# Two layers on a graph, one core: LayerNorm sums on GpSimd, the second unit turned later, the last two node tiles read first

## The chip, the cores and the metric

The kernel runs on one core of one Trainium2 chip. The metric is device time in microseconds of one execution, as the median of several runs; less is better. A NeuronCore has five engines with an instruction stream each: PE (matrix products, with a second queue PEld for the weight loads), DVE (VectorE), ACT (ScalarE), POOL (GpSimd) and SP (SyncE), which here issues nearly all DMAs. They run side by side and wait for each other by semaphores. Data lies in SBUF (128 partitions); PE writes its results to PSUM, from where DVE and ACT read them.

## What is computed

16 graphs of N = 1024 nodes with C = 256 channels, fp32. The inputs are `x` (16 x 1024 x 256), an adjacency `adj` (1024 x 1024) that all graphs share, and weights. There are two layers, and each ends in a residual sum and a LayerNorm over the channels:

```python
# layer 0
c_adj = mean(x, channels); diff = c_adj[:, None, :] - c_adj[:, :, None]
A   = abs(abs(sigmoid(diff) - 0.5) - 0.5) * 2.0
Wg  = adj * (A + A.T) * 0.5
q   = relu((x.T @ Wg) * para)                 # 4 heads of 64
k, v = split(x @ kv_w)
x   = layernorm(x + softmax(q k.T * scale) v)
# layer 1
h = relu(x @ w1_loop + adj @ (x @ w1_neigh) + b1)      # 256 -> 128
h = relu(h @ w2_loop + adj @ (h @ w2_neigh) + b2)      # 128 -> 256
x = layernorm(x + (x + h) * 0.5)
```

## The kernel before

The graphs are called batches, b = 0 to 15, and the program is a chain of them: while batch b is in its attention (layer 0), the first convolution of batch b-1 and the second of b-2 run between its parts, and the last LayerNorm of b-3. Each engine works strictly in the order in which the program text emits its instructions; nothing reorders them. A tile pool hands out buffers: 31 "row" buffers (128 x 1024 fp32) in SBUF go to one tile after the other in the order in which their last users stand in the program, and an instruction that writes a new tile waits for the last reader of the old one. PSUM is split in three "big" buffers (128 x 1024) and two "bank" buffers (128 x 512), also handed round; `half_psum` takes one half of a big one.

The large products use Strassen's scheme with seven products in place of eight, so that DVE, ACT and GpSimd have sums to prepare and to gather around each. An fp32 matmul takes two passes on PE, and both are shown as MATMUL rows.

The parts that matter here, in the order of one batch:

- **Attention, `Attention.both_units(pair)`.** A unit is a pair of heads by one half of the nodes; `both_units(0)` does units 0 and 1, `both_units(1)` units 2 and 3. `scores` multiplies kT and qT into eight tiles `s` (L757); ACT takes exp of each (L762, L764) into `pr`; DVE adds the eight up (`collect`, L776 and L778) and turns the sum in blocks of 32 x 32 to `accB` (`turned_sum`, L785). `part_sum` (L791) reduces `accB` to `den_part`, from which the softmax denominators come. `outputs` multiplies pr and v into a PSUM tile `av` (L803), which DVE turns to `o`: L828 for a pair's first unit, L835 for its second. With `summed` given (pair 0), `accB` is reduced ahead of the second unit's `outputs`; without it (pair 1) after L835.
- **`fast_inner` (L992 to L1022)**, between the two pairs: t1 = x1 times the first convolution's weights, for batch b-1, as seven products (L997) in the order 1, 2, 7, 6, 3, 4, 5, in three half PSUM tiles `upper`, `lower`, `chain`. DVE adds t1's first half behind product 2 (L1005), then runs `aside`, in most batches `turn_next`: the two transposes `xT` of the next batch's input (L253). After product 4 it adds the loop half (L1014), after product 5 L1016 and L1017, and turns t1 (L1018). Product 3 overwrites `upper`, which L1005 read. The next pair's scores take these PSUM tiles over: its first score tile the place of `upper`, its second that of `lower` (free after L1014), its fourth that of `chain` (free after L1017). Ahead of the products DVE prepares `X` by four subtractions (L984 to L987), and from batch 3 on `deviation_aside` (L1194).
- **`Joined.run`** does the two convolutions. Between its products DVE scales `o` by the denominators (L861), adds it to the blocked input xB (L863) and sums xB over 32 channels (`sum_output`, L866), and `join` (L290) adds the two halves of these sums.
- **The next batch's query products, `FastQueries`**: `times_adj` (L613) makes Wg, and four steps of seven products (L702) the query, each step over one quarter of a half's nodes. DVE gathers them in `end` (L713 and on).
- **`BlockedNorm`**, layer 0's LayerNorm, beside those steps. The data lies "blocked": partition p = (a, k), where the quarter a of 32 partitions holds other channels than its neighbour, and k stands for the node within a block of 32. A sum over all channels of a node so needs the four partition quarters added up. `fold_sums` does it by a matmul with a constant `fold` of ones on the right places (L286), whose result DVE reads from PSUM: `mean` (L356), subtracted in L359, and `variance` (L374), after ACT has squared and DVE has summed (L369, L290). GpSimd raises the variance to the power -1/2 (L376), and DVE scales with it (L381). The same `fold` adds the denominators up (L851).

For 13 batches, b = 2 to 14, the branch `elif both and more` (L1642) sets this order: `mean` goes between the fourth and fifth product of step 1, `variance` between the sixth and the last ones of step 3.

- **`ending` (L1213 to L1299)**: for the last batch the second convolution's result is finished by tiles of 128 nodes. `products` multiplies, `deviations` adds the residual (L1238), takes mean and variance (L325, L326), adds epsilon (L1241; on DVE for the last two tiles, on GpSimd for the others) and takes the power on GpSimd (L1242). Tiles 0 to 5 are normalised by ACT (L1249, `leave`), tiles 6 and 7 by DVE (L337), with one output DMA each (L1299). Their order on DVE: all of tile 6's `deviations`, all of tile 7's, then both normalisations.

Of the kernel before, what the change touches and what calls it, by code (L numbers as in the profile page):

```python
# [10 lines left out]
F32 = mybir.dt.float32  # L11
I32 = mybir.dt.int32
AF = mybir.ActivationFunctionType
ALU = mybir.AluOpType
# [4 lines left out]
def kernel(  # L19
# [31 lines left out]
    nc = tc.nc  # L51

    B, N, C = x.shape
    P = 128
    NT = N // P
# [14 lines left out]
    S = 32  # L70
# [212 lines left out]
    def fold_sums(part, name, psum_tile=bank_psum):  # L283

        pm = psum_tile(f"{name}_ps")
        nc.tensor.matmul(pm[:, 0:NB], fold.rearrange("p a k -> p (a k)"), part[:, 0, :], start=True, stop=True)  # L286
        return pm[:, 0:NB]

    def join(part):
        nc.vector.tensor_add(part[:, 0, :], part[:, 0, :], part[:, 1, :])  # L290

# [56 lines left out]
    class BlockedNorm:  # L348
# [2 lines left out]
        def __init__(self, xB, sums, name):  # L351
            self.xB, self.sums, self.name = xB, sums, name

        def mean(self):
            mean = small.tile([P, NB], F32, tag="mean", name=f"mean1_{self.name}", bufs=2)
            nc.vector.tensor_scalar_mul(mean, fold_sums(self.sums, f"sum1_{self.name}"), 1.0 / C)  # L356
            for cc in range(NC):
                x_cc = by_node(self.xB[cc])
                nc.vector.tensor_sub(x_cc, x_cc, mean.unsqueeze(2).to_broadcast([P, NB, S]))  # L359
# [9 lines left out]
                nc.vector.tensor_reduce(self.part[:, cc, :], by_node(self.sq[cc]), AX.X, ALU.add)  # L369
            join(self.part)  # L370

        def variance(self, psum_tile=half_psum):
            self.rstd = small.tile([P, NB], F32, tag="rstd1", name=f"rstd1_{self.name}", bufs=2)
            nc.vector.tensor_scalar(self.rstd, fold_sums(self.part, f"sum2_{self.name}", psum_tile), 1.0 / C, EPS,  # L374
                                    op0=ALU.mult, op1=ALU.add)
            nc.gpsimd.tensor_tensor(self.rstd, self.rstd, neg_half, ALU.pow)  # L376

        def scale(self):
# [350 lines left out]
    class Attention:  # L729
# [86 lines left out]
        def both_units(self, pair, first=lambda: None, second=lambda: None, third=lambda: None, summed=None):  # L816
            u = NJ * pair
            self.scores(u, 0)
            self.scores(u + 1, NT, summed=False)
            row = row_tile(f"o_{self.b}_{pair}")  # L820
            self.collect(u + 1, 1)
            first()
            self.collect(u + 1, 2, 3)
            second()
            self.outputs(u, half_psum, turned=False)
            self.collect(u + 1, 4, 5)
            pav, self.o[u] = self.o[u], row
            nc.vector.transpose(row[:, 0:FB], pav)  # L828
            self.collect(u + 1, 6, 7)
            accB = self.turned_sum(u + 1)  # L830
            if summed:
                summed()
                self.part_sum(u + 1, accB)
            self.outputs(u + 1, turned=False)
            nc.vector.transpose(row[:, FB:N], self.o.pop(u + 1))  # L835
            if not summed:
                self.part_sum(u + 1, accB)
            third()

        def add_pairs(self, *pairs):  # L840
            self.denominators(*pairs)
# [112 lines left out]
    class GraphConv:  # L954
# [258 lines left out]
        def ending(self, dst, quarters, aside, filled):  # L1213

            def bias(bank, *tiles):
                banks[tiles] = bank[:, 0:len(tiles) * C]
                for i, t in enumerate(tiles):  # L1220
                    banks[t] = bank[:, ts(i, C)]
                bank = bank[:, 0:len(tiles) * C].rearrange("p (i c) -> p i c", c=C)
                nc.scalar.copy(bank, b2_sb.unsqueeze(1).to_broadcast([P, len(tiles), C]))

            def products(*tiles):
                for t in tiles:
                    nc.tensor.matmul(banks[t], self.uT[:, ts(t, P)], w2n_sb, start=False, stop=False,
                                     skip_group_check=True)
                    nc.tensor.matmul(banks[t], self.h1T[:, ts(t, P)], w2l_sb, start=False, stop=True,
                                     skip_group_check=True)  # L1230

            def deviations(*tiles):
                n, rows = len(tiles), self.x[:, tiles[0]:tiles[-1] + 1, :]
                e = small.tile([P, 4 * per], F32, tag="mv_e", name=f"mv_e_{tiles[0]}", bufs=3)
                mv = e[:, 0:2 * n].rearrange("p (t s) -> p t s", s=2)
                rstd, shift = (e[:, (2 + k) * per:(2 + k) * per + n] for k in range(2))
                sums = banks[tiles[0]] if n == 1 else banks[tiles]
                nc.vector.scalar_tensor_tensor(rows, sums.rearrange("p (i c) -> p i c", c=C), 0.0, rows,  # L1238
                                               op0=ALU.max, op1=ALU.add)
                statistics(mv, rows, range(n), f"e{tiles[0]}")  # L1240
                (nc.vector if tiles[0] >= NT - 2 else nc.gpsimd).tensor_scalar_add(rstd, mv[:, :, 1], EPS2)  # L1241
                nc.gpsimd.tensor_tensor(rstd, rstd, neg_half[:, 0:n], ALU.pow)  # L1242
                return tiles, mv, rstd, shift

            def leave(tiles, mv, rstd, shift):
                nc.gpsimd.tensor_scalar_mul(shift, mv[:, :, 0], -1.0)
                nc.gpsimd.tensor_mul(shift, shift, rstd)
                for i, t in enumerate(tiles):
                    nc.scalar.activation(self.x[:, t, :], self.x[:, t, :], AF.Identity, bias=shift[:, i:i + 1],  # L1249
                                         scale=rstd[:, i:i + 1])  # L1250
                t0, n = tiles[0], len(tiles)
                nc.sync.dma_start(out=dst[t0 * P:(t0 + n) * P, :].rearrange("(t p) c -> p t c", p=P),
                                  in_=self.x[:, t0:t0 + n, :])

            per = FB // C
            half = FB // NJ
            banks, last = {}, []
            self.uT = row_tile(f"uT_{self.b}")
            upper, third = (bank_psum(f"u_ps_{self.b}_{j}") for j in range(NJ))
            fourth = half_psum(f"u_ps_{self.b}_{NJ}")  # L1260
            bias(filled[2], 6)
            bias(filled[3], 7)
            bias(filled[1], 2, 3)
            bias(filled[0], 4)
            self.neighbours(0, upper, range(NT), quarters)
            nc.scalar.copy(self.uT[:, 0:FB], upper)
            self.neighbours(1, third[:, 0:half], range(NT), quarters, slice(0, half))
            bias(upper, 0, 1)

            def copy_third():  # L1270
                nc.scalar.copy(self.uT[:, FB:FB + half], third[:, 0:half])
                bias(third, 5)

            aside(copy_third)
            products(0, 1)
            stats = deviations(0, 1)
            self.neighbours(1, fourth[:, 0:half], range(0, TJ), quarters, slice(half, FB))
            leave(*stats)
            products(2)
            stats = deviations(2)  # L1280
            products(4)
            leave(*stats)
            stats = deviations(4)
            products(5)
            fifth = deviations(5)
            self.neighbours(1, fourth[:, 0:half], range(TJ, NT), quarters, slice(half, FB))
            nc.scalar.copy(self.uT[:, FB + half:N], fourth[:, 0:half])
            leave(*stats)
            leave(*fifth)
            products(3)  # L1290
            stats = deviations(3)
            leave(*stats)
            for t in (6, 7):
                products(t)
                _, mv, rstd, _ = deviations(t)
                last.append((t, mv, rstd))
            for t, mv, rstd in last:
                normalize(mv, rstd, self.x[:, t:t + 1, :], 1)
                nc.sync.dma_start(out=dst[t * P:(t + 1) * P, :], in_=self.x[:, t, :])  # L1299

    class Joined:

# [102 lines left out]
    def run():  # L1405
# [59 lines left out]
        for b in range(B):  # L1465
# [73 lines left out]
            elif more:  # L1539
# [26 lines left out]
                    c1.load_t1()  # L1566
                    both.fetch(2, 3)

                att.both_units(0, sums, lambda: nodes.turn(), summed=summed)
                nodes.line()  # L1570
                nodes.row()
                c1.fast_inner(turn_next)
                att.both_units(1, before_convolution, third=lambda: (q.times_adj(0), q.times_adj(TJ)))
                both.left(nc.gpsimd)
                q.left(nc.gpsimd, blocked)
# [21 lines left out]
                if b + 2 < B:  # L1597
                    c2.sums_aside()
            else:
                att.both_units(0, c1.load_inner, summed=c1.inner_sums)  # L1600
                c1.fast_inner()
                att.both_units(1, third=lambda: att.add_pairs(0))
            norm = BlockedNorm(xB, att.sums, str(b))
            if more and not c1:
# [37 lines left out]
            elif both and more:  # L1642
                q.pair(2)
                q.step(0)
                q.step(1, norm.mean, 5)
                q.pair(3)
                norm.squares()
                q.step(2)
                norm.sum_squares()
                kv.load()  # L1650
                q.load_para()
                q.step(3, lambda: norm.variance(bank_psum), 4)
                qT = q.end(kv.sums, lambda: None)
                xB = load_blocked(b + 1, f"a{b + 1}")
                load_next()
# [122 lines left out]
```

## Time and profile before

| | before |
|---|---|
| median of 3 runs | 2112.22 us (2111.35 to 2114.17) |
| the profiled execution's own time | 2112.32 us |
| its span, first to last instruction | 2110.5 us |
| granted TensorE clock (mean) | 0.999 |
| one batch in the middle | 129.47 us |
| L286 fold matmuls on PE (two passes each) | 32 for means, 32 for variances |
| L374 DVE, waited for PE `sum_ps` | 20.2 us in 15 batches |
| L376 POOL, power of 128x32 | 16 of 5.5 us, 88.3 us in all |
| L791 DVE `den_part` / L835 DVE `o` | about 1.21 us / 0.71 us each |

How to read it: the profile is of one execution, whose own time stands 0.1 us from the median; its span leaves out 1.8 us around the first and last instruction. Times in the timeline count from the span's start. A row of the timeline gives start, length, engine, line of the kernel, operation, the tile written and the tiles read, shapes, and how many instructions were put together ("x4"); at the end in brackets, how long the engine stood idle before it and which instruction ended the wait. Spacings from start to start are somewhat shorter than the lengths, since an engine overlaps neighbours. A row's time on an engine that nobody waits for is not time of the kernel.

### The profile page before, as it was taken

What the parts mean: (1) busy time and instruction counts of PE and PEld (TensorE: products, weight loads), DVE (VectorE), ACT (ScalarE), POOL (GpSimd) and SP (SyncE); (2) the same over time, 40 slices, a digit from 0 to 9 for tenths busy, and PEclk for the clock granted to TensorE, in tenths of its full rate; (3) what the DMA queues carried; (4) which work ended last, traced back from release to release, by engine and by line L of the source; (5) the groups of instructions that cost most, each with busy time, mean ns of one, the idle gap of its engine ahead of it and who ended that gap; (6) DMA issues with size and microseconds to landing.
All of it is one profiled execution on the core that took longest, in us unless ns stands there. A gap on an engine that the chain in (4) does not pass through costs nothing.

```text
span 2110.5 us, 24762 instructions
## 1 busy us (share of the span) xinstructions
PE 2096.5 (99%) x8360; PEld 996.7 (47%) x8360; DVE 1890.5 (90%) x2226; ACT 1247.0 (59%) x2112; POOL 364.4 (17%) x224
## 2 busy tenths in 40 slices
PE   9999999999999999999999999999999999999998
PEld 5354434445354453544535444354443534445355
DVE  6899998989989899898998989989899898989885
ACT  5844574556756566564765747557475584655523
POOL 2011103131021311213122031210312103131022
PEclk9999999999999999999999999999999999999999
DMA  9495756766648776477865768656586564966455
GB/s 220 114 184 185 146 142 199 139 215 146 173 167 160 241 132 195 155 143 241 142 204 153 142 221 174 204 132 155 195 175 216 144 155 173 183 216 131 145 186 175
DMA packets 688694, 364.99 MB, mean 173 GB/s; under 512 B 550704, under 2 KB 629936, under 8 KB 688560
## 3 DMA queue, kind: packets, MB, share of 16 engines
q1 hardware_dynamic: 688288, 363.07, 67.0%
q8 instruction: 68, 1.11, 0.2%
q14 instruction: 66, 0.54, 0.1%
q10 hardware_dynamic: 272, 0.26, 0.0%
HBM read 305.46 MB, written 57.80 MB: 172 GB/s over the span
## 4 chain that ended last, share of the span: by engine, by line
PE 97%; DVE 2%; DMA 0%; issue 0%; SPq 0%; ACT 0%; DVEq 0%; POOLq 0%
PE s L757 21%; PE av L803 20%; PE hu_ps L1332 17%; PE g_ps L702 16%; PE v_ps L463 5%; PE k_ps L459 5%; PE in_ps L997 4%; PE hu_ps L1134 4%; PE g_ps L621 3%; DVE acc L778 1%; PE h_ps L1045 1%; PE u_ps L1074 1%; PE h_ps L1134 1%; PE t_ps L971 0%; DMA x<-in_x_dram 0%
## 5 line engine op out<-in xcount | busy, mean ns | idle before, releaser
L778 DVE TENSOR_TENSOR acc<-acc,pr 128x1024 f32<-128x1024 f32 x384 | 481.4, 1254 | 34.0 <-DVE acc L776 0.9
L757 PE MATMUL s<-qT,kT 64*128 64x512 f32 x2048 | 448.7, 592 | 0.0
L803 PE MATMUL av<-pr,v 128*64 128x512 f32 x2048 | 447.0, 594 | 0.0
L764 ACT ACTIVATE pr<-s 128x1024 f32<-128x1024 f32 x392 | 390.9, 1117 | 58.1 <-PE s L757 58.1
L757 PEld LDWEIGHTS s<-qT,kT 64*128 64x128 f32 x2048 | 195.2, 187 | 241.0 <-issue 191.2
L803 PEld LDWEIGHTS av<-pr,v 128*64 128x64 f32 x2048 | 144.0, 137 | 297.3 <-issue 269.2
L1332 PE MATMUL hu_ps<-adj,R 128*128 128x512 f32 x480 | 213.6, 592 | 0.0
L376 POOL TENSOR_TENSOR rstd<-rstd,neg_half 128x32 f32<-128x32 f32 x16 | 88.3, 5522 | 564.5 <-DVE rstd L374 564.5
L613 DVE SCALAR_TENSOR_TENSOR wg<-wg,adj 128x1024 f32<-128x1024 f32 x128 | 169.0, 1359 | 3.6 <-ACT wg L608 3.6
L762 ACT ACTIVATE pr<-s 128x512 f32<-128x512 f32 x240 | 142.5, 703 | 0.0
L607 ACT ACTIVATE wg<-c_row,c_sums 128x1024 f32<-128x1024 f32 x120 | 139.7, 1164 | 2.6 <-DVE accB L785 1.0
L1332 PEld LDWEIGHTS hu_ps<-adj,R 128*128 128x128 f32 x480 | 90.0, 190 | 107.1 <-issue 99.2
L608 ACT ACTIVATE wg<-wg 128x1024 f32<-128x1024 f32 x128 | 135.5, 1058 | 4.1
L1332 PE MATMUL hu_ps<-adj,t 128*128 128x512 f32 x240 | 109.2, 598 | 0.0
L702 PE MATMUL g_ps<-wg,x 128*128 128x512 f32 x224 | 107.7, 593 | 0.0
L702 PE MATMUL g_ps<-T,xB 128*128 128x512 f32 x208 | 107.3, 597 | 0.0
L702 PE MATMUL g_ps<-wg,xB 128*128 128x512 f32 x208 | 106.2, 592 | 0.0
L1355 ACT COPY snap<-hu_ps 128x512 f32<-128x512 f32 x15 | 8.8, 586 | 157.4 <-PE hu_ps L1332 136.1
L1195 POOL TENSOR_TENSOR rstd<-rstd,neg_half 128x8 f32<-128x8 f32 x12 | 19.6, 1637 | 457.2 <-DVE rstd L1194 457.2
L1323 POOL TENSOR_TENSOR R<-h 128x512 f32<-128x512 f32 x14 | 20.7, 1480 | 433.5 <-PE av L803 407.3
L776 DVE TENSOR_TENSOR acc<-pr,pr 128x1024 f32<-128x1024 f32 x64 | 78.0, 1219 | 14.1 <-ACT pr L764 12.9
L785 DVE STREAM_TRANSPOSE accB<-acc 128x1024 f32<-128x1024 f32 x64 | 79.7, 1245 | 3.1
(301 smaller groups left out, 3298.9 us busy)
## 6 DMA issues: line engine op xcount, KB each, us to landing
adj<-adjT SPq DMA_DIRECT2D x210, 512.0 KB
adj<-in_adj_dram SPq DMA_DIRECT2D x128, 512.0 KB
para<-in_L_gnn_para_dram SPq DMA_DIRECT2D x32, 512.0 KB
xB_a<-in_x_dram SPq DMA_DIRECT2D x128, 128.0 KB
x1d<-xB_a SPq DMA_DIRECT2D x128, 128.0 KB
x<-x1d SPq DMA_DIRECT2D x16, 1024.0 KB
xB<-in_x_dram SPq DMA_DIRECT2D x120, 128.0 KB
x<-in_x_dram SPq DMA_DIRECT2D x15, 1024.0 KB
```

Of the source, the lines that this page charges most:

```text
L459: nc.tensor.matmul(dst, self.a[0][n], self.w[n], start=not again, stop=True, skip_group_check=again)
L463: nc.tensor.matmul(dst[:, ts(t, P)], self.w[n][:, ts(t, P)], self.a[1][n], start=not again and t == 0, stop=True, skip_group_check=again o ...
L607: nc.scalar.activation(wg, self.c_row, AF.Abs, bias=self.c_col[:, t:t + 1], scale=-1.0)
L608: nc.scalar.activation(wg, wg, AF.Tanh, scale=-0.5 / C)
L613: nc.vector.scalar_tensor_tensor(wg, wg, 1.0, self.adj.pop(t), op0=ALU.add, op1=ALU.mult)
L702: nc.tensor.matmul(self.p[n], x_n[:, k, :], w_n, start=(k == 0), stop=(k == TJ - 1))
L757: nc.tensor.matmul(halves[s], self.kT[rows, pair, ts(mt, P)], self.qT[rows, pair, ts(j, FB)], start=True, stop=True)
L762: nc.scalar.activation(pr[:, ts(s, FB)], halves[s], AF.Exp)
L764: nc.scalar.activation(pr, ps, AF.Exp)
L778: nc.vector.tensor_add(self.acc, self.acc, prs[mt])
L803: nc.tensor.matmul(pav[s * HD:(s + 1) * HD, :], self.v[:, mt, pair * P + s * HD:pair * P + (s + 1) * HD], prs[mt][:, ts(s, FB)], start=(mt ...
L1332: nc.tensor.matmul(dst, self.x[n][:, k, :], of_rows(rows, k), start=(start and k == 0), stop=(k == TJ - 1), skip_group_check=again)
```

## The change

Three edits.

1. In batches 2 to 14 the four partition quarters are added up by GpSimd. The new function `across` does it in two steps. In the first it copies each half of the 64 partitions to the other half's place in the second plane of `part` and adds the planes; in the second the same with quarters of 32. That is 2 copies of 64x32, an addition of 128x32, 4 copies of 32x32, an addition of 128x32. `mean` on DVE reads the result from SBUF; the variance's scaling and epsilon (L374) move to GpSimd. `mean` and `variance` are emitted ahead of or behind whole steps instead of inside them.
2. With `summed` given, `both_units` no longer turns `o` of the second unit (L835) and reduces `accB` (L791) itself: it returns `settle`, which does both. `fast_inner` runs it as (the first) part of `aside`, that is, after t1's first half has been added (L1005) and before the `xT` transposes. On DVE the order of a batch goes from L1194, L791, L835, L1005, 2 x L253, L1014 to L1194, L1005, L835, L791, 2 x L253, L1014. This holds for the 14 batches 2 to 15. As `accB` is given back later in program order, row buffers come free in another order: the fourth adjacency load that precedes the second pair waits for another DVE row than before.
3. In `ending`, both last tiles' products are emitted first. DVE adds the residual and takes statistics of tile 6 and then 7, aggregates both, adds epsilon once for both (128x2), GpSimd takes one power of 128x2, and DVE normalises 6 and 7.

The instructions of PE, ACT and SP keep their order, apart from the 26 folds that PE loses.

```diff
+    def across(part):
+        eng = nc.gpsimd
+        for step in (2, 1):
+            n = step * S
+            for a in range(0, Q, step):
+                src = (a // step ^ 1) * n
+                eng.tensor_copy(part[a * S:a * S + n, 1, :], part[src:src + n, 0, :])
+            eng.tensor_add(part[:, 0, :], part[:, 0, :], part[:, 1, :])
+        return part[:, 0, :]
...
-        def mean(self):
+        def mean(self, joined=None):
...
-            nc.vector.tensor_scalar_mul(mean, fold_sums(self.sums, f"sum1_{self.name}"), 1.0 / C)
+            nc.vector.tensor_scalar_mul(mean, fold_sums(self.sums, f"sum1_{self.name}") if joined is None else joined,
+                                        1.0 / C)
...
-        def variance(self, psum_tile=half_psum):
+        def variance(self, psum_tile=half_psum, joined=None):
...
-            nc.vector.tensor_scalar(self.rstd, fold_sums(self.part, f"sum2_{self.name}", psum_tile), 1.0 / C, EPS,
-                                    op0=ALU.mult, op1=ALU.add)
+            (nc.vector if joined is None else nc.gpsimd).tensor_scalar(
+                self.rstd, fold_sums(self.part, f"sum2_{self.name}", psum_tile) if joined is None else joined,
+                1.0 / C, EPS, op0=ALU.mult, op1=ALU.add)
...
             if summed:
                 summed()
+            self.outputs(u + 1, turned=False)
+
+            def settle():
+                nc.vector.transpose(row[:, FB:N], self.o.pop(u + 1))
                 self.part_sum(u + 1, accB)
-            self.outputs(u + 1, turned=False)
-            nc.vector.transpose(row[:, FB:N], self.o.pop(u + 1))
-            if not summed:
-                self.part_sum(u + 1, accB)
-            third()
+                third()
+
+            if summed:
+                return settle
+            settle()
...
-            for t in (6, 7):
-                products(t)
-                _, mv, rstd, _ = deviations(t)
-                last.append((t, mv, rstd))
-            for t, mv, rstd in last:
-                normalize(mv, rstd, self.x[:, t:t + 1, :], 1)
-                nc.sync.dma_start(out=dst[t * P:(t + 1) * P, :], in_=self.x[:, t, :])
+            pair = (NT - 2, NT - 1)
+            products(*pair)
+            rows = self.x[:, pair[0]:NT, :]
...
+            for i, t in enumerate(pair):
+                nc.vector.scalar_tensor_tensor(rows[:, i, :], banks[t], 0.0, rows[:, i, :], op0=ALU.max, op1=ALU.add)
+                parts.append(small.tile([P, nc.vector.BN_STATS_DIM], F32, tag="st", name=f"st_last_{t}"))
+                nc.vector.bn_stats(parts[i], rows[:, i, :])
+            for i in range(2):
+                nc.vector.bn_aggr(mv[:, i, :], parts[i])
+            nc.vector.tensor_scalar_add(rstd, mv[:, :, 1], EPS2)
+            nc.gpsimd.tensor_tensor(rstd, rstd, neg_half[:, 0:2], ALU.pow)
+            for i, t in enumerate(pair):
+                normalize(mv[:, i:i + 1, :], rstd[:, i:i + 1], rows[:, i:i + 1, :], 1)
+                nc.sync.dma_start(out=dst[t * P:(t + 1) * P, :], in_=rows[:, i, :])
...
-                att.both_units(0, sums, lambda: nodes.turn(), summed=summed)
+                settle = att.both_units(0, sums, lambda: nodes.turn(), summed=summed)
                 nodes.line()
                 nodes.row()
-                c1.fast_inner(turn_next)
+                c1.fast_inner(lambda: (settle(), turn_next()))
...
-                att.both_units(0, c1.load_inner, summed=c1.inner_sums)
-                c1.fast_inner()
+                c1.fast_inner(att.both_units(0, c1.load_inner, summed=c1.inner_sums))
...
-                q.step(1, norm.mean, 5)
+                q.step(1)
+                norm.mean(across(att.sums))
...
-                q.step(3, lambda: norm.variance(bank_psum), 4)
+                norm.variance(joined=across(norm.part))
+                q.step(3)
```

More of the change, by code (lines that the diff above doesn't have):

```diff
@@ L1240, in deviations @@
                 statistics(mv, rows, range(n), f"e{tiles[0]}")
-                (nc.vector if tiles[0] >= NT - 2 else nc.gpsimd).tensor_scalar_add(rstd, mv[:, :, 1], EPS2)
+                nc.gpsimd.tensor_scalar_add(rstd, mv[:, :, 1], EPS2)
                 nc.gpsimd.tensor_tensor(rstd, rstd, neg_half[:, 0:n], ALU.pow)
@@ L1256, in ending @@
             half = FB // NJ
-            banks, last = {}, []
+            banks = {}
             self.uT = row_tile(f"uT_{self.b}")
@@ L1292, in ending @@
             leave(*stats)
-            for t in (6, 7):
-                products(t)
-                _, mv, rstd, _ = deviations(t)
-                last.append((t, mv, rstd))
-            for t, mv, rstd in last:
-                normalize(mv, rstd, self.x[:, t:t + 1, :], 1)
-                nc.sync.dma_start(out=dst[t * P:(t + 1) * P, :], in_=self.x[:, t, :])
+            pair = (NT - 2, NT - 1)
+            products(*pair)
+            rows = self.x[:, pair[0]:NT, :]
+            e = small.tile([P, 4 * per], F32, tag="mv_e", name="mv_e_last", bufs=3)
+            mv, rstd = e[:, 0:4].rearrange("p (t s) -> p t s", s=2), e[:, 4:6]
+            parts = []
+            for i, t in enumerate(pair):
[9 more added lines that the diff above has]
+                nc.sync.dma_start(out=dst[t * P:(t + 1) * P, :], in_=rows[:, i, :])
     class Joined:
```

## The prediction

> **What bounds the kernel now.** I read the busy times first, then the chain of waits, then the table of PE's waits, and last the timeline of the stages that the change touches. The first two say that PE is the kernel:
>
> ```profile
> span 2110.5 us, 24762 instructions
> PE 2096.5 (99%) x8360; PEld 996.7 (47%) x8360; DVE 1890.5 (90%) x2226; ACT 1247.0 (59%) x2112; POOL 364.4 (17%) x224
> PE 97%; DVE 2%; DMA 0%; issue 0%; SPq 0%; ACT 0%; DVEq 0%; POOLq 0%
> ```
>
> All PE's waits together are some 5 us, one of them in the change's stage. The batches repeat every 129.47 us (the stage's first product starts at 938.43 and at 1067.89), and PE runs through them almost without a gap.
>
> ```profile
> PE in_ps L997 <- DVE in L1005: 1.9, 1, 1.9
> ```
>
> So only two things count: PE work that disappears, and DVE results that arrive later than PE wants them. A fold of the partition sums is small, but PE pays more than its two short passes:
>
> ```profile
> 1024.06 1.02 PE L702 MATMUL g_ps<-wg,xB 128*128 128x512 f32 x2
> 1024.92 0.30 PE L286 MATMUL sum_ps<-sq_part,fold 128*128 128x32 f32 x2
> 1025.06 1.10 PE L702 MATMUL g_ps<-T,x 128*128 128x512 f32 x2
> 1026.00 1.02 PE L702 MATMUL g_ps<-T,xB 128*128 128x512 f32 x2
> ```
>
> From 1024.92 to 1026.00 there is one fold and one product of two passes, which alone takes 2 x 0.429 (1024.06 to 1024.92 is such a pair). 1.08 - 0.86 = 0.22 us (0.224 at the trace's resolution).
>
> The second unit's stage, in an ordinary batch:
>
> ```profile
> 1067.89 1.98 PE L997 MATMUL in_ps<-x1T,w1n_sb 128*128 128x512 f32 x4
> 1068.89 1.21 DVE L791 TENSOR_REDUCE den_part<-accB 128x32 f32<-128x1024 f32 x1
> 1070.02 0.71 DVE L835 STREAM_TRANSPOSE o<-av 128x512 f32<-128x512 f32 x1
> 1070.65 0.65 DVE L1005 TENSOR_TENSOR in<-in,in_ps 128x512 f32<-128x512 f32 x1
> 1071.23 2.35 DVE L253 STREAM_TRANSPOSE xT<-xB 128x1024 f32<-128x1024 f32 x2
> 1073.50 0.65 DVE L1014 TENSOR_TENSOR in<-in,in_ps 128x512 f32<-128x512 f32 x1
> 1074.13 3.27 PE L757 MATMUL s<-qT,kT 64*128 64x512 f32 x14
> ```
>
> The x4 are products 1 and 2. DVE first sums `accB`, then turns `o`, and only then adds t1's first half (L1005), although product 2 is long there. L1014 frees the PSUM buffer `lower`, which the second score tile uses: its matmul starts at 1075.09, L1014 ends at 1074.15, so there is 0.94 us of slack.
>
> **What the Trainium skill says.** "SBUF — State Buffer", section "SBUF: two separate sides", states that GpSimd and DVE share a port pair as an exclusive lock for a whole instruction, a DVE operation with two SBUF inputs taking part. The trace agrees on who collides: L613, 1.18 us each as a rule, takes 2.25 beside 128x512 GpSimd additions, while PSUM adds beside GpSimd work grow by 0.00. "GPSIMD Engine Reference", section 2.1 "Instruction dispatch", says that consecutive Pool instructions are no barrier between its cores; so each copy and add of `across` must wait for the one before. The trace has dependent small pairs, L1241 to L1242 and L1246 to L1247: 0.29 to 0.32 us from start to start. "Perfetto Trace Analysis", section "GPSIMD Instruction", trusts that spacing more than the reported duration, and I use it.
>
> **Part 1, the folds.** 13 batches (2 to 14) lose two folds each: 26 x 0.224 = **-5.83 us**, all on PE's path. In return GpSimd gets 8 small operations for each sum (16 per batch), and the epsilon step. Nearest rows: `tensor_scalar` 128x1 0.23 and `tensor_tensor` 128x1 0.19 us; 128x32 is not shown for a copy. I take 0.35 us per step for the chain, bounds 0.25 and 0.6. Both sums have to arrive in time:
>
> ```profile
> 1025.26 0.19 DVE L374 TENSOR_SCALAR rstd<-sum_ps 128x32 f32<-128x32 f32 x1 [1.42 <-PE sum_ps L286]
> 1025.53 5.44 POOL L376 TENSOR_TENSOR rstd<-rstd,neg_half 128x32 f32<-128x32 f32 x1 [32.08 <-DVE rstd L374]
> 1035.87 1.22 DVE L381 TENSOR_TENSOR xB_a<-xB_a,rstd 128x1024 f32<-128x1024 f32 x1
> ```
>
> The squares are joined at 1023.84; then 8 x 0.35 + 0.3 + 5.44 gives `rstd` at 1032.4. L381 wants it about 1034.3 to 1035.9 (the earlier if DVE keeps all the time that it saves). Hidden; at 0.6 us a step the first limit is just passed. The mean has more room: the sums are joined at 997.8 and DVE reads the mean at 1013.85, for 2.8 us of work. DVE is spared the 1.42 us in front of L374, but nothing on PE waits for DVE there, and it ends in DVE's wait for ACT before the next accumulation (1043.23). Cost and gain 0.
>
> The mean's copies do lie beside DVE work with two SBUF inputs, two L613 from 997.74 to 1000.1. Large GpSimd operations (128x128, 0.454 us alone) lengthened such a row by 0.067 to 0.083, or 0.16 for each GpSimd microsecond; a step busy for 0.19 then costs 0.03, and six of them 0.18. Behind it stand DVE results that PE wants soon: x L1138 with 0.28 us of slack, h L1156 with 0.32. About 0.16 of a slack is the signal itself (L1005 has 0.13 and is already late by 0.03). 0.18 - 0.12 = 0.06 us a batch, x13 = **+0.8**; bounds 0 (six at 0.02) and 4.7 (six at 0.08).
>
> **Part 2, the second unit behind t1.** Times from product 1's start. Product 2's last pass starts at 1.392. DVE reads a product 0.70 us after its last pass starts (L1016: 5.713 and 6.414), so t1's add starts at 2.09, not at 2.76. Product 3's wait of 0.03 us disappears: 12 x 0.03 = **-0.4**. But from 1.10 to 2.09 DVE has now nothing to do, and all the old work follows: add 0.57, `o` 0.63, `den_part` 1.13, two `xT` turns 1.13 + 1.15 (spacings of the same rows). L1014 starts at 6.70 instead of 5.61 and ends at 7.35. The second score tile would come at 7.17; it gets its buffer at 7.35 + 0.05, 0.23 late. After such a wait PE's second pass has been 0.105 later as well (batch 2's L1005 wait), which gives 0.335 at most. I take 0.29 x 12 batches (3 to 14) = **+3.5**, bounds 2.8 and 4.0. The third add, L1017, ends at 8.56 for a tile at about 8.9, and is not late. The next accumulation starts 0.4 late, and DVE's wait of 1.29 us for `av` (at 1102.07) absorbs it.
>
> Batch 2 has the one wait listed:
>
> ```profile
> 294.55 1.13 PE L997 MATMUL in_ps<-x1T,w_sums 128*128 128x512 f32 x2 [1.86 <-DVE in L1005]
> ```
>
> There three subtractions hold DVE until 292.1. With t1 directly behind them PE waits 0.4 instead of 2.16 (with its second pass), but L1014 stays where it is (same DVE work, no gap), and the score tile then waits 0.98: 1.38 in all, **-0.8**. Batch 15 has no `xT` turns and no wait: 0.
>
> **Part 3, the last two tiles.**
>
> ```profile
> 2102.48 0.43 DVE L325 BATCH_NORM_STATS2 st_e<-x 128x6 f32<-128x256 f32 x1
> 2103.52 0.58 POOL L1242 TENSOR_TENSOR mv_e<-mv_e,neg_half 128x1 f32<-128x1 f32 x1 [0.76 <-DVE mv_e L1241]
> 2104.14 0.41 DVE L337 TENSOR_SCALAR x<-x,mv_e 128x256 f32<-128x256 f32 x1 [0.44 <-POOL mv_e L1242]
> ```
>
> Tile 7's add now comes 0.6 us earlier (2101.4), its statistics end at 2102.3; two aggregations, one add, and a pow of 128x2 (0.72) give both deviations at 2103.7. Tile 6 is normalised at 2103.7 (before 2103.29), tile 7 at 2104.06. The last write starts 0.1 earlier, but the first, 0.4 later, may hold up the SP queue: -0.35 to +0.45, taken **0**.
>
> **Part 4, what moves along.** `accB` is released later, so the fourth adjacency load of a batch on SP waits for a later DVE row, about 5.6 us; two loads of `adj` and the t1 load stand behind it. Each still has several us before its reader. 0.
>
> **Sum.** -5.83 + 0.8 - 0.4 + 3.5 - 0.8 = -2.7 on the profiled execution's 2112.32 (span 2110.5 and 1.8 around it) = 2109.6. The shown median is 0.1 lower: **2109.5**. 0.2%, about what a measurement of this kernel can tell from no change, is 4.2 us.
>
> **Rivals.**
> - *The score tile doesn't wait.* If DVE's t1 add or the turns take a few tenths less than their spacings, or buffer release is faster, the 3.5 disappear, and batch 2 gains 1.7: -5.83 - 0.4 - 1.7 + 0.8 = -7.1, 2105.1. For it: only 0.2 us decide. Against: all spacings repeat to 0.01 us. Chance 0.36.
> - *GpSimd's small operations hold the port (slower).* If a small step blocks a DVE row for its full 0.19 us, as the lock's wording has it, six cost 1.1 us, less 0.12 of cover: 1.0 x 13 = 13 in place of 0.8, 2121.7. With half of it, 0.1 each, 0.48 x 13 = 6.2 and 2114.9. It turns slower than before from 0.07 per step, by 0.2% from 0.12. Against: 128x128 operations cost no more than 0.083. Chance 0.10.
> - *No gain from the folds*, because PE only waits longer elsewhere: then 5.8 of the sum goes, 2115.3. Against: no DVE or ACT wait after a fold is within 0.3 us, apart from rows that follow PE themselves. Chance 0.05.
> - The forecast: 0.49.
>
> **Range and chances.** The forecast's own bounds are 2107.5 to 2113. With the first rival and the milder part of the second: 2104.5 to 2114. Faster by over 0.2% (below 2108.0): the first rival and a fifth of the forecast, 0.45; slower by over 0.2% (above 2116.4): the harder part of the second and the worst of the third, 0.08; the rest 0.47.
>
> **What would show it.** No L286 between the g products and 0.22 us less there; L1005 at 2.09 from product 1; the second score tile at about 7.4 with a DVE release; `rstd` on GpSimd done before L381; L613 at 1.2 us beside the copies (longer: the second rival). The prediction is wrong if the tile starts at 7.17, or if L613, L1138 or L381 come later by more than 0.2 us.

## The result, and the profile after

| | before | changed |
|---|---|---|
| median of 14 runs each | 2112.02 us | 2107.70 us (2107.14 to 2109.24) |
| ratio, with its 95% interval | | 0.9979 (0.9971 to 0.9988) |
| the profiled execution's own time | 2112.32 us | 2107.44 us |
| its span | 2110.5 us | 2105.6 us |
| from PE's last matmul to the end of the span | 9.36 us | 7.70 us |

The change makes the kernel 0.2% faster: 4.3 us by the medians, 4.9 us between the two profiled executions. 2109.5 was forecast, with a range of 2104.5 to 2114. With three runs of before the forecast started from 2112.22; with all 14 its median is 2112.02. The page of the changed kernel (span, busy times, shares of the chain of waits):

```profile
span 2105.6 us, 24898 instructions
PE 2093.6 (99%) x8308; PEld 996.1 (47%) x8308; DVE 1887.9 (90%) x2212; ACT 1247.3 (59%) x2112; POOL 440.7 (21%) x444
PE 94%; DVE 5%; issue 1%; DMA 0%; DVEq 0%; SPq 0%; ACT 0%; POOLq 0%; POOL 0%
```

PE is still the kernel, with 52 matmul rows fewer (26 folds of two passes). But DVE has 5% of the chain where it had 2%: it has got a place on the path. The table of PE's waits shows only one such place:

```profile
PE s L769 <- DVE in L1030: 0.7, 1, 0.7
```

This is batch 2's second score tile (L769 is L757 of before, L1030 is L1014). The wait for L1005 in batch 2, 1.9 us, has left the table. In an ordinary batch the wait for L1030 is hidden from that table, because the time is charged to the weight load. The timeline of the stage has it (numbers in brackets: idle before, and who ended it; L1021 is L1005 of before, L848 is L835, L803 is L791):

```profile
1065.58 1.98 PE L1013 MATMUL in_ps<-x1T,w1n_sb 128*128 128x512 f32 x4
...
1066.50 0.16 DVE L1210 TENSOR_SCALAR rstd<-mv 128x8 f32<-128x8 f32 x1
...
1067.68 0.69 DVE L1021 TENSOR_TENSOR in<-in,in_ps 128x512 f32<-128x512 f32 x1 [1.01 <-PE in_ps L1013]
...
1068.28 0.71 DVE L848 STREAM_TRANSPOSE o<-av 128x512 f32<-128x512 f32 x1
...
1068.91 1.18 DVE L803 TENSOR_REDUCE den_part<-accB 128x32 f32<-128x1024 f32 x1
...
1070.01 2.36 DVE L253 STREAM_TRANSPOSE xT<-xB 128x1024 f32<-128x1024 f32 x2
...
1072.29 0.65 DVE L1030 TENSOR_TENSOR in<-in,in_ps 128x512 f32<-128x512 f32 x1
...
1072.99 0.30 PEld L769 LDWEIGHTS s<-qT,kT 64*128 64x128 f32 x4 [0.91 <-DVE in L1030]
```

DVE stands idle for 1.01 us until product 2 is there (it had summed `accB` in that time before), and all later work of the stage is 1.1 us later: L1030 starts at 6.71 from product 1, not at 5.61. The score tile comes at 7.41; with its buffer free it would have come at 7.17. A comparison of the two traces matmul by matmul gives 0.244 us for the tile's first pass and 0.104 more for the second, in each of the 12 batches 3 to 14 (0.242 to 0.245 and 0.103 to 0.105).

Where the folds were, there is a plain row of products, 0.86 us each pair:

```profile
1021.98 1.02 PE L714 MATMUL g_ps<-wg,xB 128*128 128x512 f32 x2
1022.84 1.02 PE L714 MATMUL g_ps<-T,x 128*128 128x512 f32 x2
1023.70 1.02 PE L714 MATMUL g_ps<-T,xB 128*128 128x512 f32 x2
```

GpSimd's sums come in time. Its power for the variance (L388, L376 of before) ends 2.9 us before DVE scales with the result (L393, L381 of before):

```profile
1024.62 5.44 POOL L388 TENSOR_TENSOR rstd<-rstd,neg_half 128x32 f32<-128x32 f32 x1
...
1032.95 2.36 DVE L393 TENSOR_TENSOR xB_a<-xB_a,rstd 128x1024 f32<-128x1024 f32 x2
```

Set against before, matmul by matmul, the whole difference of the spans comes apart into three:

| stretch of the span | changed minus before |
|---|---|
| up to batch 2 (load of the inputs; the same instructions in both) | -0.4 us |
| from there to PE's last matmul | -2.9 us |
| from PE's last matmul to the end | -1.7 us |

The middle one is the sum that was forecast (-2.7). The last one was not.

### The profile page after: what moved, and what is told of

Same layout as the page of the kernel before. It is cut to its first block, busy times and chain, and to the rows that moved or that the text cites. A ratio compares the mean times of both kernels' runs of the same rounds, so it can differ in the third digit from the quotient of the medians.

```text
span 2105.6 us, 24898 instructions
## 1 busy us (share of the span) xinstructions
PE 2093.6 (99%) x8308; PEld 996.1 (47%) x8308; DVE 1887.9 (90%) x2212; ACT 1247.3 (59%) x2112; POOL 440.7 (21%) x444
## 4 chain that ended last, share of the span: by engine, by line
PE 94%; DVE 5%; issue 1%; DMA 0%; DVEq 0%; SPq 0%; ACT 0%; POOLq 0%; POOL 0%
PE av L815 20%; PE s L769 20%; PE hu_ps L1358 17%; PE g_ps L714 16%; PE v_ps L475 5%; PE k_ps L471 5%; PE hu_ps L1150 4%; PE g_ps L633 3%; PE in_ps L1013 1%; DVE xT L253 1%; DVE den_part L803 1%; DVE acc L790 1%; PE h_ps L1061 1%; PE u_ps L1090 1%; PE h_ps L1150 1%
## 5 line engine op out<-in xcount | busy, mean ns | idle before, releaser
L769 PE MATMUL s<-qT,kT 64*128 64x512 f32 x2048 | 452.4, 594 | 1.6 <-DVE in L1030 0.7
L769 PEld LDWEIGHTS s<-qT,kT 64*128 64x128 f32 x2048 | 199.0, 187 | 242.6 <-issue 179.3
L625 DVE SCALAR_TENSOR_TENSOR wg<-wg,adj 128x1024 f32<-128x1024 f32 x128 | 168.3, 1354 | 3.6 <-ACT wg L620 3.6
L388 POOL TENSOR_TENSOR rstd<-rstd,neg_half 128x32 f32<-128x32 f32 x16 | 88.3, 5520 | 147.2 <-DVE rstd L385 146.1
```

Source lines behind the costliest of these rows:

```text
L625: nc.vector.scalar_tensor_tensor(wg, wg, 1.0, self.adj.pop(t), op0=ALU.add, op1=ALU.mult)
L769: nc.tensor.matmul(halves[s], self.kT[rows, pair, ts(mt, P)], self.qT[rows, pair, ts(j, FB)], start=True, stop=True)
```

## The experiments

Ten kernels, with 5 to 21 runs each. Each was timed beside runs of the kernel before on the same chip, and the ratio is to those: their median was 2113.03 us beside the first four kernels of the table, 2112.62 beside the next four and 2111.91 beside the last two. So medians from different groups compare only to about 1 us. "Loop" is the time from batch 2 to PE's last matmul, against before; "tail" is from there to the end of the span (before: 9.36 us). Both are read from one profiled execution of each kernel.

| kernel | median us | ratio to before, 95% interval | loop | tail |
|---|---|---|---|---|
| part 1 alone | 2106.89 | 0.9972 (0.9961 to 0.9983) | -4.2 | 8.98 |
| part 2 alone | 2114.04 | 1.0006 (0.9998 to 1.0015) | +3.0 | 8.12 |
| part 3 alone | 2112.10 | 0.9998 (0.9990 to 1.0007) | +1.5 | 9.53 |
| changed, `accB` reduced first | 2103.75 | 0.9958 (0.9945 to 0.9972) | -6.9 | 7.54 |
| changed, one `xT` turn behind L1030 | 2103.46 | 0.9957 (0.9943 to 0.9971) | -7.6 | 7.86 |
| both of these | 2105.40 | 0.9966 (0.9954 to 0.9979) | -6.9 | 9.33 |
| before, 23 small DMAs more | 2111.40 | 0.9995 (0.9987 to 1.0004) | 0.0 | 8.22 |
| changed, 16 more copies per mean | 2107.83 | 0.9977 (0.9968 to 0.9986) | -2.9 | 8.15 |
| changed, 115 small DMAs more | 2109.65 | 0.9987 (0.9980 to 0.9993) | -2.9 | 8.96 |
| before, part 2 in batch 2 alone | 2111.02 | 0.9996 (0.9988 to 1.0004) | -0.8 | 9.09 |

**The three parts, each alone.** The edits are the parts of the change's diff: `across` and its uses; `settle` and its uses; the end of `ending`.

> Only part 1 (sums by GpSimd). My account: 26 folds at 0.224 us leave PE and the copies cost DVE nothing that PE sees, so -5.8 us to about 2106.2; the 0.03 us wait for the add behind product 2 stays. Rival (copies hold the port, DVE late before the next batch's query products): -5.8 plus up to 5, 2107 to 2111. Second question: does the stretch from PE's last matmul to the end (9.4 us before, 7.7 after) stay at 9.4, as the ending is the old one? If it falls to about 7.7 here too, it isn't part 3 that shortened it.

> Only part 2 (second unit behind t1's first half). My account: second score tile 0.35 us late in 12 batches (+4.2), no wait at product 3 (-0.4), batch 2 shorter by 0.8: +3.0 us, about 2115.0, slower than before. Rival (the move is what it looks like, a wait taken off PE, and pays by itself): 2111.5 or less.

> Only part 3 (last two tiles read first). Theory A: the end after PE's last matmul falls from 9.4 to 7.7 us because of the new order, so -1.6 us, about 2110.4. Theory B: DVE and POOL finish at most 0.25 us earlier, and the rest of the 1.6 us is where the fetch of instructions falls at the end, which this edit need not move: 2111.5 to 2112.3.

Part 1 alone is 6.1 us faster than the runs of before beside it; its interval overlaps with that of the whole change. Its loop of -4.2 is -5.8 for the 26 folds and 1.7 of something else, which the table of stretches of this kernel shows (columns: from and to, length, busy time of PE, PEld, DVE, ACT and POOL with counts, the granted TensorE clock, DMA share, GB/s):

```profile
290.00:293.00 3.00, 2.13 (x5) 0.49 (x3) 2.93 (x5) 1.33 (x3) 0.00 (x0) 1.00 0.00 0
293.00:295.00 2.00, 1.01 (x2) 0.63 (x3) 2.00 (x3) 0.00 (x0) 0.00 (x0) 0.87 0.00 0
295.00:296.00 1.00, 1.00 (x2) 0.34 (x1) 1.00 (x2) 0.34 (x1) 0.00 (x0) 0.50 0.00 0
296.00:297.00 1.00, 1.00 (x2) 0.34 (x1) 0.21 (x1) 0.24 (x1) 0.00 (x0) 0.50 0.00 0
```

This is batch 2, just after PE has waited 1.86 us for t1's add. The clock is at 0.50 for 3.41 us, and the products take twice as long: 1.7 us. The kernel before has the same wait, and in its profiled execution the clock stayed at 1.00. So the 1.7 us are not a cost of part 1. Part 1 leaves this wait where it was; part 2 takes it away.

Part 2 alone loses: +3.0 in the loop, as worked out for it. Its short tail gives 1.2 us back. That its median is then only 1.0 above that of before may be due to the half clock of batch 2, which some runs of before pay and part 2 takes away; that is not shown. The rival, that the move pays by itself, falls. Part 3 alone makes no change in time that these runs can tell, and its tail is the long one, 9.53; its loop of +1.5 is again 1.7 us of half clock in batch 2, in a loop whose instructions are those of before. So theory A for the tail falls: part 2 alone has a short tail with the old ending, part 3 alone a long one with the new.

**What makes the score tile late.** The changed kernel with the reduction back in front:

```diff
             if summed:
                 summed()
+                self.part_sum(u + 1, accB)
             self.outputs(u + 1, turned=False)
 
             def settle():
                 nc.vector.transpose(row[:, FB:N], self.o.pop(u + 1))
-                self.part_sum(u + 1, accB)
+                if not summed:
+                    self.part_sum(u + 1, accB)
                 third()
```

> The changed kernel with accB's reduction (1.13 us) put back ahead of t1's add, into the 1 us in which DVE has nothing to do; only the turn of o stays behind t1. My account: t1's add starts at 2.13 instead of 2.09, the loop half's add back at 5.6 instead of 6.71, the second score tile waits for nothing: 12 x 0.35 = -4.2 against the changed kernel, about 2103.5. Rival (the tile is late for another reason, the row buffers handed out in another order): no change, 2107.7.

Its timeline (L803 is the reduction, L1023 t1's add, L1032 the loop half's add):

```profile
1065.07 1.21 DVE L803 TENSOR_REDUCE den_part<-accB 128x32 f32<-128x1024 f32 x1
1066.20 0.68 DVE L1023 TENSOR_TENSOR in<-in,in_ps 128x512 f32<-128x512 f32 x1
1066.79 0.71 DVE L849 STREAM_TRANSPOSE o<-av 128x512 f32<-128x512 f32 x1
1067.43 2.33 DVE L253 STREAM_TRANSPOSE xT<-xB 128x1024 f32<-128x1024 f32 x2
1069.68 0.65 DVE L1032 TENSOR_TENSOR in<-in,in_ps 128x512 f32<-128x512 f32 x1
```

No gap in front of the add, and the score tile waits for nothing: 2103.75, 4 us below the changed kernel (4.2 expected; in batch 2 PE waits 1.3 us for t1's add again). The reduction fits into the hole: the add starts at 2.11 us from product 1, in the changed kernel at 2.10, and the loop half's add at 5.59 in place of 6.71. The second way keeps the change's order, but lets L1030 past one of the transposes:

```diff
             product(4, lower, again=True)
             nc.vector.tensor_add(self.loops[:, 0:FB], u2, lower)
+            later()
...
-                c1.fast_inner(lambda: (settle(), turn_next()))
+                c1.fast_inner(lambda: (settle(), turn_next()),
+                              lambda: nc.vector.transpose(xT_next[:, 1, :], blocked[1]))
```

where `turn_next` now makes `xT_next` and turns its first half only.

> The changed kernel, but the second of the two xT transposes goes behind the loop half's add. My account: that add starts at 5.6 from product 1's start instead of 6.7, the second score tile waits for nothing (-4.2), and in batch 2 it comes 1.1 us earlier as well, so its 0.7 us wait there goes too: about 2102.7. Rival (whatever DVE does later just moves the wait to the fourth score tile, which takes the place of chain): 2106 or more, with a wait of PE for the add that frees chain.

It has 2103.46, 0.8 above what was expected, and no wait of PE for the loop half's add. What batch 2 was to give is there in part (PE waits 0.2 us there for the add that frees `chain`, which is the rival, in one batch only). This and the kernel before it are the fastest of the study, and their intervals overlap: both beat the change by some 4 us.

> Both mends: accB's reduction ahead of t1's add, and the second xT transpose behind the loop half's add. In an ordinary batch either of them is enough, so nothing is added up: loop as in the kernel with the reduction first, about 2103.7, batch 2 with its 1.3 us wait at product 3. If it is over 1 us faster than both others, something else than the second score tile's wait was in play.

The loop is as expected, -6.9. The time, 2105.40, is 1.7 and 1.9 us worse than with either of the two alone. Against the reduction first this is all tail, 9.33 against 7.54. Against the turn behind the add it is 1.5 us of tail and 0.7 us of loop, since batch 2 has PE's wait of 1.3 us for t1's add back.

**The tail.** After the last write of the output has been issued, SP branches over a part of the program that isn't run, as all engines do, and then waits for the DMA queues, eight waits in a row. The span ends 1.91 us after the first of these waits in ten of the twelve profiles (2.09 us in part 2 alone and in the kernel with the reduction first). The instructions of that line in the kernel before and then in the changed one (columns: count, length in ns, first and last start):

```profile
L1723 SPq EVENT_SEMAPHORE  x8: 17/17/17, 2108.6 to 2109.2; - x8
...
L1723 SPq COMPARE_BRANCH  x1: 50/50/50, 2105.9 to 2105.9; - x1
```

```profile
L1750 SPq EVENT_SEMAPHORE  x8: 17/17/17, 2103.7 to 2104.2; - x8
...
L1750 SPq COMPARE_BRANCH  x1: 50/50/50, 2102.4 to 2102.4; - x1
```

From the branch to the first wait it is 2.73 us before, 1.24 us in the changed kernel. The last write had reported 0.9 us ahead of that first wait before, and 0.09 us ahead of it in the changed kernel; the queue that the first wait is for had reported much earlier in both, 0.24 us ahead of the branch and 0.15 us behind it. So SP was not held up by the DMAs there. What differs on SP is the number of its instructions: 1718 ahead of the branch before, 1741 in the changed kernel (without the five that open every one of these programs). The 23 more are waits on semaphores; the DMAs are as many as before. Part 2 alone has them, parts 1 and 3 alone don't: they come with the row buffers that part 2 gives back later. The first trial of this adds to the kernel before, in batch 8,

```diff
+                if b == 8:
+                    spare = dram.tile([1, 32], F32, tag="spare", name="spare", bufs=1)
+                    for i in range(23):
+                        nc.sync.dma_start(out=spare[0:1, i:i + 1], in_=ident[0:1, 0:1])
```

> The kernel before with 23 DMAs of 4 bytes added on SP in batch 8, so that SP's program is as long as the changed kernel's (1741 instructions ahead of the final branch instead of 1718). Theory: where SP's last instructions lie decides whether SP must wait for them behind the branch; the time from SP's branch to its first wait falls from 2.7 us to about 1.2 or less, and the kernel gets 1.3 us faster at the same loop (before's median of this call minus 1.3). Rival: SP's length has nothing to do with it, 2.7 us and no change within 0.3 us.

1.51 us from branch to wait, and a tail of 8.22. The median is 1.2 below that of before, but its interval holds no change, so the time alone doesn't settle it. The opposite trial does more: the changed kernel with nine such DMAs in each of the batches 2 to 13 and seven in batch 14, so that SP's program ends 115 instructions later.

> The changed kernel with 115 DMAs of 4 bytes more on SP, nine in a batch, so that its program has 1856 instructions ahead of the final branch. So far 1718 and 1730 waited 2.5 to 2.7 us behind the branch, 1741 and 1743 only 0.5 to 1.5. If what counts is where the last instructions lie in blocks of 128 (8192 bytes, the size of the instruction fetches in the trace), 1856 stands where 1728 does, and the long wait comes back: 2.5 us or more, tail of 9.2 us or more, 1 to 1.6 us slower than the changed kernel, about 2109. Rival (a longer program is as good): 1.5 us or less, 2107.7. The loop should not change.

The loop is unchanged, the wait is back at 2.51 us, the tail at 8.96 (9.2 was expected), and the median at 2109.65; the fastest of its 21 runs, 2108.32, is slower than 13 of the changed kernel's 14. The tail accounts for 1.3 us of the 1.9 between the two medians; the rest is not explained. All kernels together, by SP's length:

| SP instructions ahead of the branch | branch to first wait, us |
|---|---|
| 1718 (before, part 1 alone, part 3 alone) | 2.73, 2.55, 2.71 |
| 1719 (part 2 in batch 2 alone) | 2.57 |
| 1730 (reduction first and one turn later) | 2.62 |
| 1856, that is 1728 + 128 | 2.51 |
| 1741 (changed, part 2 alone, one turn later, 23 DMAs, 16 copies) | 1.24, 1.22, 0.69, 1.51, 0.98 |
| 1743 (reduction first) | 0.49 |

That SP's length decides, and not by its size alone, is what these numbers show: the two kernels that only add DMAs to SP went the way that was expected of their length, no kernel is out of line, and 1856 is slow again. That the waits repeat with every 128 instructions rests on this one kernel and is not shown. That it is the fetch of the instructions behind the branch fits well. In each of the six long tails the trace has an instruction DMA of 8192 bytes that starts 0.93 to 0.95 us after SP's branch, and the first wait follows 1.6 to 1.8 us after its start; none of the short tails has one there before its first wait. That this DMA is SP's own the trace doesn't say, so this part stays argued.

**The shared port.** In the changed kernel behind `across(att.sums)`:

```diff
+                joined = across(att.sums)
+                for i in range(16):
+                    nc.gpsimd.tensor_copy(att.sums[0:2 * S, 1, :], att.sums[2 * S:P, 0, :])
+                norm.mean(joined)
```

> The changed kernel with 16 more GpSimd copies of 64x32 behind each batch's sum for the mean, beside the DVE work whose results PE wants within 0.3 us. As the trace of the changed kernel has it, GpSimd waits for DVE there and not the other way round: DVE rows stay within 0.02 us, no change, 2107.7. Rival (a small copy holds DVE for 0.03 to 0.1 us): 13 batches x 0.3 to 1 us, 2111 to 2120, with PE waits at the two convolutions' last products.

2107.83: no change, no new PE wait. The rival falls. One DVE row beside the added copies takes 0.72 in place of 0.69 us, a little more than was expected. The changed kernel's trace shows who pays instead (the first two copies of `across` beside L625, which is L613 of before):

```profile
995.89 2.37 DVE L625 SCALAR_TENSOR_TENSOR wg<-wg,adj 128x1024 f32<-128x1024 f32 x2
```

```profile
996.10 2.22 POOL L295 COPY sums<-sums 64x32 f32<-64x32 f32 x2 [4.51 <-DVE sums L300]
998.40 0.25 POOL L296 TENSOR_TENSOR sums<-sums 128x32 f32<-128x32 f32 x1
998.72 1.42 POOL L295 COPY sums<-sums 32x32 f32<-32x32 f32 x4
```

Each of the two copies takes 1.1 us; the same copies for the variance, beside a DVE row that has one of its inputs in PSUM, take 0.2 us:

```profile
1022.12 0.45 POOL L295 COPY sq_part<-sq_part 64x32 f32<-64x32 f32 x2 [21.65 <-DVE sq_part L300]
```

DVE's two rows take 2.37 us, before, beside an idle GpSimd, 2.35 us.

**Batch 2 alone.** `settle` is returned for batch 2 only; in the other batches the old order stays.

> The kernel before with the second unit moved behind t1's first half in batch 2 alone. The loop gets 0.8 us shorter. If PE's 1.9 us wait in batch 2 is also what makes TensorE run at half clock for a while in part of the executions (1.7 us, as in two profiles so far), then the upper group of the runs of before (2112.8 to 2114) has no counterpart here: nearly all runs within 1 us from about 2110.9, median about 1.2 to 1.5 below that of before. Rival (the two groups have another cause): two groups here as well, each 0.8 lower. SP's program has 1719 instructions, so the tail stays long.

The loop is 0.8 shorter, as expected. The median is 0.9 below that of before. 11 of 13 runs lie between 2110.5 and 2111.8, two above (2112.7 and 2113.4); of before's 33 runs beside them 22 lie between 2111.2 and 2112.2 and 11 above 2113. This leans towards the theory, but two runs of 13 against 11 of 33 don't settle it. The other kernels point both ways: of the 38 runs of three kernels that also lack the wait (changed, part 2 alone, 16 more copies) only three lie more than 1 us above their kernel's median, but of the 13 runs of before with 23 DMAs, which has the wait, only one does.

## Why the prediction was right

Its own steps, against what the runs showed:

| step | forecast | shown |
|---|---|---|
| 26 folds | -5.83 | -5.80 (26 x 0.223 in the trace) |
| GpSimd copies beside DVE | +0.8 | 0 |
| wait for L1005 at product 3 | -0.4 | -0.4 (12 x 0.033) |
| second score tile | +3.5 (2.8 to 4.0) | +4.2 (12 x 0.348) |
| batch 2 | -0.8 | -0.8 (-1.73 + 0.84 + 0.10) |
| last two tiles | 0 (-0.35 to +0.45) | 0 in time, with part 3 alone |
| what moves along on SP | 0 | about -1.5, in the tail |

- The folds' price, read from the spacing of two products in place of the rows' own lengths, is right to a hundredth: in each of the 26 places PE saves 0.14 us for the two passes and 0.08 us at the product behind them. Nothing took their place: GpSimd's eight steps for a variance took 2.19 us, 0.27 each, where 0.35 was taken, and `rstd` was there 2.9 us early.
- The second score tile's wait is right in place, cause and sign; its size is just over the upper bound. The term that was mis-sized is the second pass, 0.105 later: it was seen in one place, taken at a half, and holds in every batch. The first rival, that this wait doesn't bite, is out: the add started at 6.71 and ended at 7.36, where 6.70 and 7.35 were worked out.
- One step that failed is the price of GpSimd's small operations, 0.03 us of DVE each. It scaled down what 128x128 operations had cost. The section "SBUF: two separate sides" of "SBUF — State Buffer" in the Trainium skill says that whichever operation starts first has the pair for the whole instruction and the other one fully blocks; the trace agrees: L625 started first, and GpSimd stood still for 0.9 us of each copy's 1.1, while DVE lost no more than 0.02 us a row. Which of the two loses was not asked in the prediction; here it was GpSimd, whose sums were ready 11.5 us before DVE read the mean, in spite of that. (The 2.25 us that the prediction gives for L613 beside large additions are 2.28 to 2.29 in the trace; nothing hangs on it.)
- "What moves along" was costed at nothing, by the slack of the loads. That was right for the loads: no PE wait for data is new. It left out that SP's own instructions become more, and where they end. This is the other step that failed, and nearly all of the 1.8 us between forecast and result. That the loop comes out so close, -2.9 for -2.7, is luck in part: the score tile (0.7 too low) and the copies (0.8 too high) cancel each other.
- Part 3: the last write was issued 0.14 us earlier from PE's last matmul (3.75 to 3.61 us), where 0.1 was forecast. Over all profiles it is 3.55 to 3.86 us with the old ending and 3.28 to 3.61 with the new one. The time with part 3 alone didn't change, since the span's end hangs on SP's first wait.

So the change is 7.0 us of gains on PE (folds 5.8, product 3's wait 0.4, batch 2 0.8), 4.2 us of a new wait in twelve batches, and some 1.5 us less at the end that come from SP's length, a side effect of part 2 that nobody aimed at. As a change of order part 2 loses; the same intention, t1's add ahead of `o`, without the hole in front of it, keeps the whole gain of part 1 and adds 1.0 us in the loop. The other 2 us by which the median of the kernel with the reduction first lies below that of part 1 alone (2103.75 and 2106.89) are 1.4 us of tail and perhaps the half clock of batch 2, which part 1 alone can still meet.

## What to carry to other kernels

When an instruction is brought forward on an in-order engine, ask first when its operand is there: if it must now wait, everything queued behind it moves back by the hole, and the first buffer that comes free too late is the new wait. Fill the hole with the work that was ready, and leave the rest behind. A small matmul between two large ones cost PE more here than its two passes, 0.22 us in place of 0.14; GpSimd with slack could take such sums, also beside DVE work that kept it waiting. And compare the end of the program apart from its loop: in this kernel 1 to 2 us there came and went with edits far away.

## What the runs showed of the hardware

- After PE's wait of 1.86 us in batch 2 the granted clock was 0.50 for 3.41 us in two profiled executions (part 1 alone, part 3 alone), and stayed at 1.00 in two others with the same wait (before, and before with 23 DMAs). It costs 1.7 us. "TensorE: Matmul & The Clock Gate" in the Trainium skill, section "Part 1: The HAM clock gate (the "warmup" mystery)", gives half clock after an idle window of about 3.4 us; here a little over half of that was enough, in two of four profiles.
- A GpSimd copy of 64x32 took 0.2 us beside a DVE operation with an input in PSUM, and 1.1 us beside one with two SBUF inputs (L625) that had started first. The DVE rows were longer by up to 0.02 us, and one by 0.03 with 16 more copies.
- From SP's last branch to its first wait it took 2.5 to 2.7 us with 1718, 1719, 1730 and 1856 SP instructions ahead of the branch, and 0.5 to 1.5 us with 1741 and 1743, in one profile of each of twelve kernels.
